# A scale by 1/sqrt(D) goes from a pass over a weight tile to ScalarE's evacuations, and two modulation rows go to two periods

## The chip, the cores and the metric

The kernel runs on one core of one Trainium2 chip. The metric is device time of one execution in microseconds (us), as the median of the timed runs. The program is one launch; the host only lays the inputs out.

The engines of the core are named as the profile names them: PE (TensorE matmuls), PEld (TensorE's weight loads), DVE (VectorE), ACT (ScalarE), POOL (GpSimd) and SP (SyncE, whose queue issues the DMAs here).

## The reference, cut to what matters

Two blocks run one after the other on x of shape 2 x 2048 x 512 (two sequences, L = 2048 positions, D = 512 features). The first is an S5 block with a feed-forward. The second is attention between two modulated layer norms, with 16 heads of 32 features. The change is in the second block alone:

```python
def _L1_cond_ref(hidden, w, ...):
    h = _sln(hidden, w, ln_g, ln_b, Wg, bg, Wb, bb)      # layer norm, then gamma * ln + beta
    q, k, v = split of (h @ Wqkv.T + bqkv) into 16 heads of 32
    energy = jnp.einsum('bhqd,bhkd->bhqk', q, k)
    att = jax.nn.softmax(energy, axis=-1) / D ** 0.5     # the 1/sqrt(D) stands after the softmax
    out = jnp.einsum('bhqk,bhkd->bhqd', att, v)
    out = out @ Wp.T + bp
    h1 = out + hidden
    h2 = _sln(h1, w, ln_g, ln_b, Wg, bg, Wb, bb)         # the same gamma and beta again
    return h2 + h1
```

So 1/sqrt(D), named ISQ in the kernel, is a plain factor on the attention's output. It may be multiplied in anywhere between the softmax and the projection by Wp. The last layer norm needs two rows of 512 numbers for each sequence: a scale (gamma times ln_g) and a shift (gamma times ln_b, plus beta).

## The kernel before

The first stage, up to about 1390 us, runs the S5 block and the feed-forward chunk by chunk, and computes keys, queries and values. The attention stage comes after it and fills the rest.

The attention stage handles 64 blocks. A block `n` is a sequence `b`, a pair of heads `p` and a chunk `c` of 512 queries. Each block has 16 key tiles of 128 keys, and scores are held transposed: keys along the partitions, 2 heads x 512 queries along the row. The softmax subtracts the true maximum of each query, so a block's maxima must be complete before its first exponential:

- `keep` (L867, L872): PE makes a score tile `s` in PSUM, ACT copies it to SBUF as `x`, and DVE takes the running maximum `run`. Eleven of the 16 tiles of a block are treated so. `compare` (L876) only takes the maximum of the other five.
- `turn_run` and `spread` (L884 to L898): the maxima are transposed on PE, reduced on DVE, sent to DRAM and read back spread over all partitions as `shift`.
- `take_off` (L904): POOL adds `shift` to each of the eleven kept tiles. `make` (L910): PE recomputes the five others, and DVE adds `shift`, giving `pT`.
- `exponentials` (L915): ACT takes the exponential of each tile, in place.
- `weighted` (L925): PE multiplies the exponentials with the values into one PSUM bank `o`. The weights hold the values and a block of ones, so rows 0 to 31 of `o` are the output of the even head, rows 32 to 63 its sum, rows 64 to 95 the sum of the odd head and rows 96 to 127 its output. After the last tile of a block ACT copies `o` to `raw` (L934), and SP writes the sums and the outputs to DRAM (`sd` at L938, `od` at L941). There are 63 such copies; the last block of all ends in `end_last` instead.

A hand-written order sets who follows whom: the program is recorded in periods `j`, eight to a block (`NP = 8`), and each engine executes its instructions in the order in which they were recorded. `after(j, ...)` puts a piece of work at the head of period `j`, `closing(j, ...)` puts it behind that period's exponentials. Scores run 14 periods ahead of their use (`AHEAD`). All DMAs go through SP's queue, in order.

What the change and the steps below it touch:

- `wp`, the projection's weights, is loaded in period 2 * NP + 6. In period 4 * NP (head of block 4) POOL multiplies the whole tile, 128 x 2048, by ISQ in place (L1328).
- `last_rows(b)` makes the two modulation rows of sequence `b` with `along_rows` (L170, L174): matmuls of a broadcast column against the identity into the PSUM bank "pt", then an ACT copy to SBUF. There is one "pt" bank, and `turn_run`, `spread` and the projections use it too. `last_rows` is called twice, by `after`: for the first sequence (`b` = 0) at the head of block 34, and for the second (`b` = LB) at the head of period `j + 2`, where `j` is the period after the one in which the last head pair's first chunk is complete.
- `fetch`, `divide`, `project`, `residual`, `statistics` and so on (L979 to L1080) take finished chunks through the division by the sums, the projection and the last norm. For the first sequence this is spread over the second sequence's blocks; for the second it comes at the end.
- `end_last` finishes the last block: its outputs go straight from PSUM to the projection without the way through DRAM. It divides by the sums with one reciprocal and two multiplications for each half (L1162, L1164).

Of the kernel before, what the change touches and what calls it, by code (L numbers as in the profile page):

```python
# [8 lines left out]
F32 = mybir.dt.float32  # L9
# [4 lines left out]
AF = mybir.ActivationFunctionType  # L14
# [5 lines left out]
P = 128  # L20
# [19 lines left out]
def tile_s5_block_then_sln_attention(  # L40
# [125 lines left out]
    def along_rows(dst, cols, psum, tag):  # L166

        pt = psum.tile([P, CH], F32, name="pt_ar", tag=tag)
        for k in range(KC):
            nc.tensor.matmul(  # L170
                pt[:, k * P : (k + 1) * P], cols[k].to_broadcast([P, P]), ident,
                start=True, stop=True,
            )
        nc.scalar.copy(dst, pt)  # L174
# [743 lines left out]
    def weighted(n, kt, first, final):  # L918

        if first:  # L920
            outs[n] = ps_o.tile([P, CH], F32, name="o")
        x = probs.pop((n, kt))
        v = vst[pair_of[n] % 2]
        for e in range(2):
            nc.tensor.matmul(  # L925
                outs[n][64 * e : 64 * e + 64, :], v[:, kt, e : e + 2, :], x[:, e, :],
                start=first, stop=final,
            )
        if final and n == len(blocks) - 1:
            end_last(outs.pop(n))  # L930
        elif final:
            b, p, c = blocks[n]
            raw = work.tile([P, CH], F32, name="raw", bufs=1)
            nc.scalar.copy(raw, outs.pop(n))  # L934
            cols = slice(c * CH, (c + 1) * CH)
            for e in range(2):
                j = 2 * p + e
                nc.sync.dma_start(sd[b][j : j + 1, cols], raw[32 + 32 * e : 33 + 32 * e, :])  # L938
            for e in range(2):
                j = 2 * p + e  # L940
                nc.sync.dma_start(od[b][HD * j : HD * j + HD, cols], raw[96 * e : 96 * e + 32, :])  # L941
# [1 line left out]

    held, ending = {}, {}

    def last_rows(b):
        g_row = rows.tile([P, D], F32, name="g_row", bufs=1)
        along_rows(g_row, [s_scale[:, k, b : b + 1] for k in range(KC)], ps, "pt")
        t_row = rows.tile([P, D], F32, name="t_row", bufs=1)
        along_rows(t_row, [s_shift[:, k, b : b + 1] for k in range(KC)], ps, "pt")  # L950
        ending[b] = g_row, t_row

    def fetch_sums(b, c, heads=slice(0, NH), width=64):

# [196 lines left out]
    def end_last(o):  # L1151
        raw, inv = (spare(n)[:, 0, :] for n in ("raw4", "inv4"))
        on = ends["o"][1][:, 1, :]
        turned = ps.tile([P, 2, 2 * P], F32, name="turned", tag="pt")
        parts = [slice(2 * i * P, 2 * (i + 1) * P) for i in range(2)]
        for at in parts:
            nc.scalar.copy(raw[:, at], o[:, at])
        end_begin(1)
        for i, at in enumerate(parts):
            nc.tensor.matmul(turned[:, i, :], ends["turn"], raw[:, at], start=True, stop=True)  # L1160
        for i, at in enumerate(parts):
            nc.vector.reciprocal(inv[:, at], turned[:, i, :])  # L1162
            for r in (slice(0, HD), slice(3 * HD, P)):
                nc.vector.tensor_tensor(on[r, at], o[r, at], inv[r, at], ALU.mult)  # L1164
        end_project(1, list(range(NG - 1)))
        mv = small.tile([P, TT, 2], F32, name="mv4")
        g_row, t_row = ending[LB]
        for i in range(2):
            for t in (2 * i, 2 * i + 1):
                nc.tensor.matmul(  # L1170
                    ends["py", i][:, t % 2, :], on[:, t * P : (t + 1) * P], ends["w"], start=False, stop=True
                )
            for t in (2 * i, 2 * i + 1):
                st = small.tile([P, 6], F32, name="st3")
                nc.vector.bn_stats(st, ends["py", i][:, t % 2, :])
                nc.vector.bn_aggr(mv[:, t, :], st)
        v = small.tile([P, TT], F32, name="v4")
        scale = small.tile([P, TT], F32, name="scale4")
        nc.vector.tensor_scalar(v, mv[:, :, 1], EPS, None, ALU.add)
        nc.vector.tensor_scalar(  # L1180
            scale.bitcast(I32), v.bitcast(I32), -0.5, float(0x5F3759DF), ALU.mult, ALU.add
        )

        nc.gpsimd.tensor_scalar(v, v, -0.5, None, ALU.mult)
        for _ in range(3):
            c = small.tile([P, TT], F32, name="c4")
            nc.gpsimd.tensor_tensor(c, scale, scale, ALU.mult)
            nc.gpsimd.tensor_tensor(c, c, v, ALU.mult)
            nc.gpsimd.tensor_scalar(c, c, 1.5, None, ALU.add)
            nc.gpsimd.tensor_tensor(scale, scale, c, ALU.mult)  # L1190
        ws, hts = [spare("w01"), spare("w23")], [spare("ht01"), spare("ht23")]
        for t in range(TT):
            h = ends["py", t // 2][:, t % 2, :]
            w, ht = ws[t // 2][:, t % 2, :], hts[t // 2][:, t % 2, :]
            nc.vector.scalar_tensor_tensor(w, h, mv[:, t, 0:1], g_row, ALU.subtract, ALU.mult)
            nc.vector.tensor_tensor(ht, h, t_row, ALU.add)
        for t in range(TT):
            qt = LC * TT + t
            w, ht = ws[t // 2][:, t % 2, :], hts[t // 2][:, t % 2, :]
            nc.vector.scalar_tensor_tensor(ht, w, scale[:, t : t + 1], ht, ALU.mult, ALU.add)  # L1200
            nc.sync.dma_start(out[LB, qt * P : (qt + 1) * P, :], ht)
# [47 lines left out]
    for b in range(NB):  # L1249
        for c in range(NQ):  # L1250
            j = NP * (blocks.index((b, NPAIR - 1, c)) + 1) + 1
            if (b, c) == (LB, LC):
                most, rest = slice(0, NH - 4), slice(NH - 4, NH - 2)
                j = NP * (N - 1)
                after(j - 5, fetch_sums, b, c, most)
                after(j - 3, invert, b, c, most)
                for g in range(NG - 1):
                    after(j - 2 + g, end_sums, g)
                after(j + 1, end_weights)
                after(j + 1, end_sums_more)  # L1260
                after(j + 2, end_x)
                after(j + 1, fetch_sums, b, c, rest, 32)
                after(j + 4, invert, b, c, rest, 32)
                after(j + 5, end_divisors, NG - 1, 2, 1)
                for g in range(NG - 1):
                    after(j + 3 + g, end_divide, g)
                for e in (1, 2):
                    after(j + 8, end_divide, NG - 1, slice(HD * e, HD * e + HD))
                after(j + 6, end_begin, 0)
                for g in range(NG - 1):  # L1270
                    after(j + 6 + g // 2, end_project, 0, [g])
                continue
            after(j, fetch_sums, b, c)
            after(j + 2, invert, b, c)
            if c == 0:
                after(j + 2, last_rows, b) if b == LB else after(NP * (NPAIR * NQ * (b + 1) + 2), last_rows, b)
            for t in range(TT):
                qt = c * TT + t
                if b == LB:
                    k = j + 3 + 2 * t  # L1280
                    after(k, fetch, b, qt)
                    after(k + 2, divide, b, qt)
                    after(k + 3, project, b, qt)
                    after(k + 3, residual, b, qt)
                    after(k + 3, statistics, b, qt)
                    after(k + 4, deviation, b, qt)
                    after(k + 5, last_norm, b, qt)
                    after(k + 6, last_close, b, qt)
                else:

                    k = NP * (NPAIR * NQ * (b + 1) + 2 + 3 * qt // 2)
                    after(k, fetch, b, qt)
                    after(k + 3, divide, b, qt)
                    for g in range(NG):
                        closing(k + 5 + g // 2, project, b, qt, (g,))
                    closing(k + 7, residual, b, qt)
                    closing(k + 8, statistics, b, qt)
                    closing(k + 9, gain, b, qt)
                    after(k + 11, turns, b, qt)
                    closing(k + 12, scaled, b, qt)  # L1300
                    after(k + 14, close, b, qt)
# [9 lines left out]
    for j in range(FIRST, NP * N + 2):  # L1311
# [12 lines left out]
            wp = fixed.tile([P, KC, D], F32, name="wp")  # L1324
        if j == 2 * NP + 6:
            nc.sync.dma_start(wp, w_pT.rearrange("(k p) f -> p k f", p=P))
        if j == 4 * NP:
            nc.gpsimd.tensor_scalar(wp, wp, ISQ, None, ALU.mult)  # L1328
        run_due(j)
        n, i = block_at(j + AHEAD)  # L1330
        todo = list(keeps[i]) if n is not None else []
# [90 lines left out]
```

## Time and profile before

| | |
|---|---|
| median of 3 runs | 3393.38 us (3393.34 to 3394.49) |
| the profiled execution | 3393.83 us |
| its span, first to last instruction | 3392.1 us |
| TensorE clock granted over the span | 0.992 |
| PE busy | 3294.7 us (97%) |
| POOL busy | 2117.6 us (62%) |
| ACT busy | 1951.0 us (58%) |
| DVE busy | 2218.2 us (65%) |
| the scale pass L1328 | 5.369 us, once, at 1531.7 us |
| a copy `raw` L934 | 588 ns, 63 times |
| an exponential L915 of a kept tile | 1059 ns, 704 times |
| a copy `x` L867 | 1011 ns, 704 times |
| an addition L904 on POOL | 2390 ns, 704 times |

The shares of busy time are means over two stages. In the first stage PE is busy and the other engines have much time to spare; in the attention stage all four compute engines are busy for most of each block. So the cost of an instruction is read from the stretch in which it stands. A steady block can be timed by the starts of two `raw` copies that follow each other: most of those of the first sequence are 28.1 us apart.

### The profile page before, as it was taken

How to read it: one execution, taken by the hardware profiler on the slowest of the kernel's cores; microseconds unless marked ns; L12 is line 12 of the kernel's file. 1: busy time of each engine (PE TensorE's matmuls, PEld its weight loads, DVE VectorE, ACT ScalarE, POOL GpSimd, SP SyncE). 2: the span in 40 equal slices, each digit the busy share in tenths (PEclk: the TensorE clock that was granted, in tenths of full speed). 3: DMA queues.
4: the chain of work that ended last, by engine and by line, in shares of the span. 5: the costliest groups of instructions: out<-in, count | busy, mean ns of one | idle time of the engine just before them, and what ended most of it. 6: DMA issues, size and time to landing. Idle time of an engine off the chain costs nothing.

```text
span 3392.1 us, 33637 instructions
## 1 busy us (share of the span) xinstructions
PE 3294.7 (97%) x11076; PEld 1417.8 (42%) x11076; DVE 2218.2 (65%) x2792; ACT 1951.0 (58%) x2210; POOL 2117.6 (62%) x1164
## 2 busy tenths in 40 slices
PE   7999999999999999999999999999999999999987
PEld 4444444444444444443444444444444434443432
DVE  5352525252525212688888888888888888888884
ACT  2111111111111111598999999999888888888852
POOL 2341313131313111399999999999899999989885
PEclk9999999999999999999999999999999999999998
DMA  8022221222222212332313231323233243243233
GB/s 298 25 50 71 53 75 49 78 57 71 62 62 56 59 47 75 113 85 61 74 49 74 67 74 49 75 68 75 70 92 90 67 95 88 65 90 83 63 102 97
DMA packets 249781, 259.07 MB, mean 76 GB/s; under 512 B 94920, under 2 KB 167112, under 8 KB 245510
## 3 DMA queue, kind: packets, MB, share of 16 engines
q1 hardware_dynamic: 249606, 256.92, 28.5%
q8 instruction: 88, 1.44, 0.2%
q14 instruction: 87, 0.71, 0.1%
HBM read 166.77 MB, written 67.76 MB: 69 GB/s over the span
## 4 chain that ended last, share of the span: by engine, by line
PE 62%; DVE 15%; ACT 15%; issue 3%; POOL 2%; DMA 2%; SPq 0%; DVEq 0%; ACTq 0%; POOLq 0%
PE ph L538 13%; PE po L551 13%; PE o L925 10%; DVE run L872 8%; PE s L856 8%; ACT x L867 7%; PE pk L587 6%; ACT x L915 4%; ACT pT L915 4%; PE pv L599 3%; DVE pT L910 3%; PE py L1005 2%; POOL x L904 2%; DVE run L876 2%; PE pu L474 2%
## 5 line engine op out<-in xcount | busy, mean ns | idle before, releaser
L904 POOL TENSOR_TENSOR x<-x,shift 128x1024 f32<-128x1024 f32 x704 | 1654.9, 2390 | 134.1 <-DMA shift<-flat 117.1
L856 PE MATMUL s<-qs,ks 128*128 128x512 f32 x2688 | 824.8, 427 | 39.4 <-DVE run L872 26.6
L867 ACT COPY x<-s 128x1024 f32<-128x1024 f32 x704 | 692.2, 1011 | 142.9 <-PE s L856 137.1
L872 DVE TENSOR_TENSOR run<-s,run 128x1024 f32<-128x1024 f32 x576 | 705.2, 1224 | 81.7 <-ACT x L867 37.1
L915 ACT ACTIVATE x<-x 128x1024 f32<-128x1024 f32 x704 | 738.8, 1059 | 15.7 <-POOL x L904 15.4
L925 PE MATMUL o<-x,v 128*64 128x512 f32 x2816 | 717.2, 611 | 1.2 <-ACT x L915 1.2
L856 PEld LDWEIGHTS s<-qs,ks 128*128 128x128 f32 x2688 | 444.1, 189 | 454.7 <-DVE run L872 158.0
L538 PE MATMUL ph<-fT,w_sb 128*128 128x512 f32 x1024 | 459.4, 592 | 0.9 <-ACT fT L682 0.9
L551 PE MATMUL po<-w_sb,hid 128*128 128x512 f32 x1024 | 460.0, 592 | 0.0
L542 ACT ACTIVATE hid<-ph,vec 128x512 f32<-128x512 f32 x128 | 87.8, 686 | 614.7 <-PE ph L538 614.7
L910 DVE TENSOR_TENSOR pT<-s,shift 128x1024 f32<-128x1024 f32 x320 | 388.9, 1215 | 52.6 <-PE s L856 52.2
L876 DVE TENSOR_TENSOR run<-s,run 128x1024 f32<-128x1024 f32 x320 | 389.3, 1216 | 12.1 <-PE s L856 11.6
L915 ACT ACTIVATE pT<-pT 128x1024 f32<-128x1024 f32 x320 | 339.5, 1061 | 89.9 <-DVE pT L910 89.6
L561 POOL TENSOR_TENSOR x<-x,gated 128x512 f32<-128x512 f32 x32 | 39.6, 1269 | 506.5 <-DVE gated L560 506.5
L925 PE MATMUL o<-pT,v 128*64 128x512 f32 x1280 | 332.0, 597 | 15.2 <-ACT pT L915 15.2
L164 DVE SCALAR_TENSOR_TENSOR lo<-pk,vec,hi 128x512 fp32r<-128x512 f32 x64 | 47.8, 746 | 423.0 <-ACT hi L163 423.0
L551 PEld LDWEIGHTS po<-w_sb,hid 128*128 128x128 f32 x1024 | 194.4, 190 | 243.9 <-issue 243.7
L538 PEld LDWEIGHTS ph<-fT,w_sb 128*128 128x128 f32 x1024 | 194.1, 190 | 243.3 <-issue 239.2
L925 PEld LDWEIGHTS o<-x,v 128*64 128x64 f32 x2816 | 157.0, 135 | 311.7 <-issue 239.3
L163 ACT ACTIVATE hi<-pk,vec 128x512 fp32r<-128x512 f32 x64 | 44.0, 687 | 373.4 <-PE pk L587 373.4
L524 POOL TENSOR_TENSOR x<-x,gated 128x512 f32<-128x512 f32 x28 | 35.4, 1264 | 255.3 <-DVE gated L523 255.3
L925 PEld LDWEIGHTS o<-pT,v 128*64 128x64 f32 x1280 | 91.6, 138 | 200.2 <-issue 142.2
(280 smaller groups left out, 2449.3 us busy)
## 6 DMA issues: line engine op xcount, KB each, us to landing
ks<-kd SPq DMA_DIRECT2D x128, 256.0 KB
qs<-qd SPq DMA_DIRECT2D x512, 64.0 KB
shift<-flat SPq DMA_DIRECT2D x64, 512.0 KB
moved<-fT SPq DMA_DIRECT2D x224, 64.0 KB
x<-in_x SPq DMA_DIRECT2D x8, 1024.0 KB
w_sb<-in_w SPq DMA_DIRECT2D x8, 1024.0 KB
kd<-hi SPq DMA_DIRECT2D x32, 256.0 KB
kd<-lo SPq DMA_DIRECT2D x32, 256.0 KB
```

The costliest lines, as they stand in the source:

```text
L538: nc.tensor.matmul(ph, w1_sb[:, k, f * P : (f + 1) * P], fts[b, c][:, k, :], start=k == 0, stop=k == KC - 1)
L551: nc.tensor.matmul(pos[b, c][:, t, :], hid[:, t * P : (t + 1) * P], w2_sb[:, f, :], start=f == 0, stop=f == FC - 1,)
L587: nc.tensor.matmul(pk, w[:, k, g * P : (g + 1) * P], hT[:, k, :], start=k == 0, stop=k == KC - 1)
L599: nc.tensor.matmul(pv, fts[b, c][:, k, t * P : (t + 1) * P], wv[:, k, :], start=k == 0, stop=k == KC - 1)
L856: nc.tensor.matmul(s[:, e, :], kst[pair_of[n], e][:, kt * P : (kt + 1) * P], qst[n][:, e, :], start=True, stop=True,)
L867: nc.scalar.copy(x, s)
L872: nc.vector.tensor_tensor(runs[n], s, kept[n, 0] if kt == 1 else runs[n], ALU.max)
L876: nc.vector.tensor_tensor(runs[n], raw_scores(n, kt), runs[n], ALU.max)
L904: nc.gpsimd.tensor_tensor(x, x, shifts[n], ALU.add)
L910: nc.vector.tensor_tensor(x, s, shifts[n], ALU.add)
L915: nc.scalar.activation(x, x, AF.Exp)
L925: nc.tensor.matmul(outs[n][64 * e : 64 * e + 64, :], v[:, kt, e : e + 2, :], x[:, e, :], start=first, stop=final,)
```

## The change

Three things are done.

1. The pass of POOL over `wp` (L1328) is taken out. A column `by_row` of 128 numbers takes its place: ISQ on the 64 partitions that hold outputs, 1.0 on the 64 that hold sums. ACT's evacuation of `o` to `raw` becomes an activation Identity with `by_row` as its scale, one factor for each partition. POOL fills the column once, with three memsets.
2. `end_last`, which does not pass through `raw` for its outputs, multiplies by ISQ in its division: `scalar_tensor_tensor` in place of `tensor_tensor`, four times.
3. `last_rows` becomes `last_row`, which makes one row. The two rows are recorded behind the exponentials of two successive periods by `closing`, no more both at the head of one by `after`. For the second sequence they also come up to two periods earlier (`j` and `j + 1`, where it was `j + 2`).

```diff
@@ weighted
-            nc.scalar.copy(raw, outs.pop(n))
+            nc.scalar.activation(raw, outs.pop(n), AF.Identity, scale=by_row)
@@
-    def last_rows(b):
-        g_row = rows.tile([P, D], F32, name="g_row", bufs=1)
-        along_rows(g_row, [s_scale[:, k, b : b + 1] for k in range(KC)], ps, "pt")
-        t_row = rows.tile([P, D], F32, name="t_row", bufs=1)
-        along_rows(t_row, [s_shift[:, k, b : b + 1] for k in range(KC)], ps, "pt")
-        ending[b] = g_row, t_row
+    by_row = small.tile([P, 1], F32, name="by_row", bufs=1)
+    nc.gpsimd.memset(by_row, ISQ)
+    for i in (1, 2):
+        nc.gpsimd.memset(by_row[HD * i : HD * i + HD], 1.0)
+
+    def last_row(b, name, columns):
+        row = rows.tile([P, D], F32, name=name, bufs=1)
+        along_rows(row, [columns[:, k, b : b + 1] for k in range(KC)], ps, "pt")
+        ending.setdefault(b, []).append(row)
@@ end_last
-                nc.vector.tensor_tensor(on[r, at], o[r, at], inv[r, at], ALU.mult)
+                nc.vector.scalar_tensor_tensor(
+                    on[r, at], o[r, at], ISQ, inv[r, at], ALU.mult, ALU.mult
+                )
@@ the plan
-                after(j + 2, last_rows, b) if b == LB else after(NP * (NPAIR * NQ * (b + 1) + 2), last_rows, b)
+
+                k = j if b == LB else NP * (NPAIR * NQ * (b + 1) + 2)
+                closing(k, last_row, b, "g_row", s_scale)
+                closing(k + 1, last_row, b, "t_row", s_shift)
@@ the loop over periods
-        if j == 4 * NP:
-            nc.gpsimd.tensor_scalar(wp, wp, ISQ, None, ALU.mult)
```

## The prediction

> **What bounds the kernel now.** I read the page first, then the windows from one `raw` copy to the next, then the timeline at each of the three places that the change touches, and last the groups by form for durations. From the page:
>
> ```profile
> span 3392.1 us, 33637 instructions
> PE 3294.7 (97%) x11076; PEld 1417.8 (42%) x11076; DVE 2218.2 (65%) x2792; ACT 1951.0 (58%) x2210; POOL 2117.6 (62%) x1164
> ```
>
> The shares of POOL and ACT hide that the attention stage loads all four engines. The windows show it (columns: stretch, length, then PE, PEld, DVE, ACT and POOL busy, granted clock, DMA share, GB/s):
>
> ```profile
> 1506.66:1534.79 28.13, 27.83 (x116) 11.54 (x115) 24.76 (x23) 26.66 (x31) 26.25 (x11) 1.00 0.14 43
> 1534.79:1567.76 32.97, 29.00 (x118) 11.51 (x116) 24.76 (x23) 26.62 (x30) 29.48 (x13) 1.00 0.38 90
> 1567.76:1596.09 28.33, 27.68 (x115) 11.36 (x114) 24.75 (x23) 26.62 (x30) 27.67 (x13) 1.00 0.20 55
> ...
> 2357.60:2388.94 31.34, 30.36 (x134) 13.51 (x132) 24.75 (x23) 27.84 (x32) 30.16 (x14) 1.00 0.26 69
> ```
>
> A normal block takes 28.13 us with PE busy for 27.83, ACT for 26.66 and POOL for 26.25 of them. So a few microseconds put into one engine's order in one place cannot be made up: they move the end. The second and fourth rows are two blocks in which that happens.
>
> **Part 1, the pass over wp.** The timeline at the second row:
>
> ```profile
> 1526.85 4.74 POOL L904 TENSOR_TENSOR x<-x,shift 128x1024 f32<-128x1024 f32 x2 [1.80 <-DMA shift<-flat]
> ...
> 1531.68 5.37 POOL L1328 TENSOR_SCALAR wp<-wp 128x2048 f32<-128x2048 f32 x1
> ...
> 1537.13 21.08 POOL L904 TENSOR_TENSOR x<-x,shift 128x1024 f32<-128x1024 f32 x9
> ...
> 1539.53 1.06 ACT L915 ACTIVATE x<-x 128x1024 f32<-128x1024 f32 x1 [4.16 <-POOL x L904]
> ```
>
> POOL cannot start a block before its shift lands, and the pass sits behind the second of eleven additions. Without it the third would end at 1531.59 + 2.38 = 1533.97; its exponential, one block (28.13) after that of 1507.12, would be due at 1535.25. So POOL has 1.28 to spare, and the pass costs 5.37 - 1.28 = 4.1: ACT's idle 4.16. With the refilling of the pipeline the block is 32.97 - 28.13 = 4.84 longer, and the next 28.33 - 28.13 = 0.20, part of which other blocks with key loads show too (28.35 at 1905.51). Gain 4.95. What is late next at that place is PE, as in any block. The Trainium skill (GPSIMD Engine Reference, section 4.1) calls one-input elementwise work on GpSimd "roughly line-rate"; with its 128 fp32 a cycle (section 3) and 1.2 GHz that is an estimate of 2048 / 1.2 = 1.7 us for this pass, so a delay of only 0.4, and the whole sum below would be 3.6. The row says 5.369 and ACT's wait confirms it, so I take the trace.
>
> **Part 2, the rows.** Before, both at once:
>
> ```profile
> 2381.71 1.16 PE L170 MATMUL pt_ar<-ident,s_scale 128*128 128x128 f32 x8
> 2382.91 0.59 ACT L174 COPY g_row<-pt_ar 128x512 f32<-128x512 f32 x1 [0.90 <-PE pt_ar L170]
> 2383.55 1.16 PE L170 MATMUL pt_ar<-ident,s_shift 128*128 128x128 f32 x8 [0.68 <-ACT g_row L174]
> 2384.46 1.63 PE L856 MATMUL s<-qs,ks 128*128 128x512 f32 x6
> ...
> 3200.23 1.16 PE L170 MATMUL pt_ar<-ident,s_scale 128*128 128x128 f32 x8 [1.29 <-DVE neg L885]
> ...
> 3202.98 1.62 PE L856 MATMUL s<-qs,ks 128*128 128x512 f32 x6
> ```
>
> The second row needs the one "pt" bank, so PE stands until ACT has copied the first. First pair: PE gives 2384.46 - 2381.71 = 2.75 to it, and the block is 31.34 - 28.13 = 3.21 longer. Second pair: it stands behind `turn_run`, whose bank DVE still reads, so PE waits for that as well; the scores of 3202.98 would have begun 0.41 after the transposes of 3198.28, so PE loses 4.29. Some returns: from the `raw` before it to `pt_neg` it is 3210.24 - 3191.89 = 18.35, and in a block with the same reciprocal (L963) 2315.44 - 2300.56 = 14.88. Excess 3.47.
>
> After, by the program's order, the first row stands behind six scores and the second behind the next block's first six (for LB, behind the six and then the four of two successive periods). No wait is left: the bank's earlier users are periods away, and the first row's copy is recorded before `raw`, ahead of the second row's matmuls. What stays is PE's work, 2384.46 - 2383.55 = 0.91 for a row, since the row is eight records and not the transposes' four. ACT's copy, 0.46 from start to start, lies beside it. In the first pair about 0.3 of the first row vanishes in PE's own waits for DVE at the block's end (0.23 at 1507.53 in a normal block); the rest falls where PE ends last. So 1.5 stays in the first pair and 1.8 in the second: gains 3.21 - 1.5 = 1.7 and 3.47 - 1.8 = 1.7. The price of a row lies between 0.46 (only ACT's copy shows) and 1.3 (both add up), so each gain between 0.7 and 2.5.
>
> **Part 3, 63 evacuations with a factor.** No row has this form. The nearest:
>
> ```profile
> 1506.66 0.58 ACT L934 COPY raw<-o 128x512 f32<-128x512 f32 x1
> 1507.12 1.08 ACT L915 ACTIVATE x<-x 128x1024 f32<-128x1024 f32 x1
> ...
> 1508.36 1.01 ACT L867 COPY x<-s 128x1024 f32<-128x1024 f32 x1 [0.16 <-PE s L856]
> ...
> L1053 ACT ACTIVATE o<-o,scale 128x512 f32<-128x512 f32 x16 | 11.5, 722 | 0.0
> L1072 ACT ACTIVATE z<-xr,shift,scale 128x512 f32<-128x512 f32 x12 | 9.3, 779 | 3.2 <-DVE neg L885 3.1
> ```
>
> L1053 has the same function and a scale by partition, from SBUF: 722 ns, and 0.61 to the next start (2468.59 to 2469.20). The copy takes 588, and 0.46 to the next. So +0.14 by 63, 8.8 us more of ACT; upper bound L1072 with two columns, 0.72 to the next, +0.26; lower bound nothing. Is it on the path? The exponential behind `raw` is used a period later. The copy behind that waits 0.16 for PE, and back-to-back ACT instructions overlap by about 0.1 here, so it has about 0.25 to spare. PE's next product into `o` starts at 1508.20, and `raw` is done at 1507.24. So +0.14 is hidden; in a few blocks (2482.15) the copy follows at once, and I charge 0.1 in all. At +0.26 little would show either. The rule that speaks against the change is in the Trainium skill (ScalarE: Activation LUTs, What ACT_TABLE_LOAD costs): each [128,1] pointer operand adds about 93 ns. Over 63 that is 5.9 us, and with ACT as the limit the sum would be 2.2. The idle 0.16 before the copy decides for hidden. The function needs no table load: the program's order has three loads before and after.
>
> **The small rest.** `end_last`'s four multiplications are on the final chain: 742 (L1047, this form) against 681 (L1048, the old one) for 512 columns, so at most 0.24; I take 0.2, not below nothing. The memsets are three of 0.10 (L1413) in a POOL order that stands 49.07 us idle before L1323: nothing, 0.3 if that cover were gone. The writes of `sd` and `od` go out 0.14 later, and on SP's queue the query loads behind them, which run blocks ahead: nothing. SP's and DVE's orders are else unchanged. The projection now waits for wp's load (issued 1495.3) and not for POOL, first at 2404: nothing. `by_row` slides the SBUF tiles behind it by 32 bytes; L915 takes 1059 on `x`, whose tiles start at odd multiples of 32, and 1061 on `pT`, at multiples of 64: nothing.
>
> **The sum.** -4.95 - 1.7 - 1.7 + 0.1 + 0.2 = -8.05 against the profiled execution's 3393.83 (3392.1 of span and 1.7 around it). That execution is 0.45 above the median and inside the runs' range; so from the median 3393.38 it gives 3385.3.
>
> **The rivals.** (a) ACT is the limit after all, and the longer `raw` comes through. For: ACT is back to back from `pT` to the next copies in each block. Against: the idle before the copy. At 0.09 to 0.14 each it gives 5.7 to 8.8 back: 3391.0 to 3394.1, within 0.2%. (b) Splitting the rows saves nothing, since PE's work is the same and the restart is paid twice. For: ACT's copy of the second row lies where DVE waits 2.06 for ACT's copies. Against: 0.68 and 1.29 us of waits go. Then -4.95 + 0.3: 3388.7. (c) Slower: the evacuation costs more than any near row shows, say by reading `o` from PSUM with a factor. The place is the copy behind the exponential; beyond 0.25 more than the copy each extra counts 63 times. It cancels the gain at 0.25 + 8.05 / 63 = 0.38 and is slower by over 0.2% from 0.49; at 0.5 it is +15.8 - 8.05, so 3401.1. For: no row has the form. Against: PSUM rows with two columns (L156) take 778 to 811 ns.
>
> **How the numbers follow.** 0.2% is 6.8 us, about what a measurement of this kernel can tell from no change. The sum is likeliest, 0.74, with a range of its own of 3383 to 3388 (part 2's bounds and 0.3 on part 1): 0.64 of it below 3386.6 and 0.10 above. (a) has 0.10, (b) 0.09, (c) 0.07. The range 3382.5 to 3390.5 takes in the sum's range, (b) and a small part of (a), and leaves out (c). Faster 0.64, within 0.2% 0.29, slower 0.07.
>
> **What would show it.** Right: L1328 gone; the `raw` starts at 1534.79 and the next about 28.1 apart; no wait of PE for `g_row`, and eight records of L170 in four places without idle before them; `raw` at 690 to 720 ns, with the copy two places behind it still waiting for PE. Wrong: blocks of the first sequence 0.1 longer than 28.13 throughout with that idle gone (a); the blocks with rows still above 30.5 (b); `raw` above 900 ns (c).

## The result: 3384.49 us, and the profile after

The changed kernel takes 3384.49 us as the median of 8 runs (3382.16 to 3387.56), and the kernel before takes 3393.36 us beside it (8 runs, 3390.28 to 3397.74). The ratio is 0.9977, with a 95% interval of 0.9968 to 0.9987. That is 8.87 us less, where the prediction's sum was 8.05 us less. The profiled execution of the change, the fastest of the eight, took 3382.16 us, with a span of 3380.4.

From the page of the change:

```profile
span 3380.4 us, 33642 instructions
PE 3285.9 (97%) x11076; PEld 1416.0 (42%) x11076; DVE 2217.5 (66%) x2792; ACT 1957.1 (58%) x2210; POOL 2111.1 (62%) x1166
```

PE, PEld and DVE execute as many instructions as before. ACT has gained 6.1 us, which is 63 evacuations at 0.103 each (6.5) to within half a microsecond. POOL has two instructions more, three memsets for one pass. The shares of busy time have hardly moved, so again they say nothing of where the time went.

The windows from one `raw` to the next say it. The columns are stretch, length, then PE, PEld, DVE, ACT and POOL busy, granted clock, DMA share, GB/s. The second and fourth rows are the two blocks that were 32.97 and 31.34 long:

```profile
1504.35:1532.45 28.10, 27.78 (x116) 11.54 (x115) 24.73 (x23) 26.74 (x30) 26.68 (x12) 1.00 0.15 43
1532.45:1560.58 28.13, 27.84 (x116) 11.55 (x115) 24.59 (x23) 26.75 (x30) 25.17 (x12) 1.00 0.48 116
1560.58:1588.86 28.28, 27.81 (x116) 11.55 (x115) 24.92 (x23) 26.73 (x30) 26.36 (x12) 1.00 0.15 45
2349.94:2378.51 28.57, 28.26 (x123) 12.23 (x122) 25.21 (x23) 27.20 (x31) 26.77 (x12) 1.00 0.29 73
2378.51:2410.47 31.96, 31.96 (x133) 14.70 (x134) 24.98 (x24) 27.27 (x32) 29.91 (x14) 1.00 0.39 79
3181.74:3217.07 35.33, 33.72 (x139) 14.90 (x138) 27.57 (x36) 27.71 (x32) 31.93 (x15) 1.00 0.35 103
```

Before, the windows of the last two of these blocks read:

```profile
2388.94:2420.39 31.45, 30.80 (x123) 12.94 (x122) 25.35 (x24) 26.65 (x30) 27.16 (x13) 1.00 0.39 80
3191.89:3228.84 36.95, 33.82 (x139) 14.84 (x138) 27.64 (x36) 27.62 (x33) 30.61 (x15) 1.00 0.36 98
```

Below, a block's number is that of the `raw` copy at its end, counted from 1 (the kernel counts from 0), so these are blocks 5, 34, 35 and 61. Block 5 has lost 32.97 - 28.13 = 4.84. Blocks 34 and 35 together have lost 62.79 - 60.53 = 2.26: one row of the pair has moved into block 35, which is 0.51 longer, and block 34 is 2.77 shorter. Block 61 has lost 1.62. From the first `raw` to the 62nd it is 1826.11 before (1450.06 to 3276.17) and 1816.64 after (1447.77 to 3264.41): 9.47 less, of which these three places are 8.72.

Not all of the 4.84 is the pass. The prediction saw 4.16 of idle time on ACT in block 5 and took the other 0.68 for the refilling of the pipeline. The end of that block before, in ACT's and then in SP's timeline, shows another cause:

```profile
1564.04 1.06 ACT L915 ACTIVATE x<-x 128x1024 f32<-128x1024 f32 x1 [0.86 <-POOL x L904]
```

```profile
1553.83 0.27 SPq L896 DMA_DIRECT2D flat<-neg_row  x1
1556.99 0.34 SPq L898 DMA_DIRECT2D shift<-flat  x1
```

The read `shift` of the next block goes out 3.16 us after the write `flat`. The usual gap is 1.3 (median of 64 in this trace). So POOL's next additions came late in this one execution, and ACT waited for them once more. Three other runs told below keep the pass and have no late read there; in them block 5 is 31.91 to 32.22, and the pass costs 3.8 to 4.1.

What lies ahead of the first `raw` is not the change either. POOL's first instruction of the attention stage, the memset of `v`, starts at 1405.59 before and at 1403.44 after, with the same work in the same order ahead of it, but for the three short memsets of `by_row`. The first 100 us differ in the clock column, before and then after:

```profile
0.00:100.00 100.00, 79.19 (x367) 46.12 (x368) 58.70 (x231) 22.78 (x34) 22.91 (x40) 0.93 0.70 254
```

```profile
0.00:100.00 100.00, 78.83 (x372) 45.67 (x373) 58.94 (x231) 23.36 (x35) 25.10 (x42) 0.95 0.71 256
```

By this column the twelve traces of this document fall into two groups, whatever the kernel. In six it is 0.93, and the memset of `v` starts at 1405.6 to 1407.2; in six it is 0.95 to 0.97, and the memset starts at 1403.4 to 1404.0. That the clock is the cause is likely but not shown. The run of the change that is told last below had 0.93, and its first `raw` at 1449.90, as before. So of the 11.7 us between the two spans some 7.7 are the change, some 2 are the first stage, 1.05 is the late read, and the rest is small.

Where the pass stood, POOL now goes on with its additions (the timeline of POOL, then of ACT, in the change):

```profile
1524.42 21.17 POOL L904 TENSOR_TENSOR x<-x,shift 128x1024 f32<-128x1024 f32 x9 [1.42 <-DMA shift<-flat]
...
1533.03 1.07 ACT L915 ACTIVATE x<-x 128x1024 f32<-128x1024 f32 x1
```

Nine additions follow each other behind the landing of `shift`. The exponential of the third, which waited 4.16 us for POOL, comes directly behind `raw` with no idle time at all.

The two rows of the first pair, in PE's timeline of the change:

```profile
2374.04 1.65 PE L856 MATMUL s<-qs,ks 128*128 128x512 f32 x6
2375.53 1.05 PE L170 MATMUL pt_ar<-ident,s_scale 128*128 128x128 f32 x8
2376.52 1.08 PE L925 MATMUL o<-x,v 128*64 128x512 f32 x4
...
2379.89 1.05 PE L170 MATMUL pt_ar<-ident,s_shift 128*128 128x128 f32 x8
2380.87 1.94 PE L925 MATMUL o<-x,v 128*64 128x512 f32 x8
```

Each row takes 0.98 to 0.99 from its start to PE's next work, and neither has idle time before it. In the second pair there is one new wait, of a transposition for the bank that ACT is still reading:

```profile
3189.64 0.59 ACT L174 COPY t_row<-pt_ar 128x512 f32<-128x512 f32 x1
...
3190.28 0.66 PE L884 MATMUL pt_run<-ident,run 128*128 128x128 f32 x4 [0.28 <-ACT t_row L174]
```

The evacuation, from the list of the tile `raw` on ACT (min/median/max in ns):

```profile
L934 ACT ACTIVATE raw<-o,by_row x63: 668/691/713, 1447.8 to 3307.1; 128x512 f32<-128x512 f32 x63
```

### The profile page after: what moved, and what is told of

Same layout as the page of the kernel before. It is cut to its first block, busy times and chain, and to the rows that moved or that the text cites. A ratio compares the mean times of both kernels' runs of the same rounds, so it can differ in the third digit from the quotient of the medians.

```text
span 3380.4 us, 33642 instructions
## 1 busy us (share of the span) xinstructions
PE 3285.9 (97%) x11076; PEld 1416.0 (42%) x11076; DVE 2217.5 (66%) x2792; ACT 1957.1 (58%) x2210; POOL 2111.1 (62%) x1166
## 4 chain that ended last, share of the span: by engine, by line
PE 62%; ACT 16%; DVE 13%; DMA 3%; issue 3%; POOL 2%; SPq 1%; ACTq 0%; DVEq 0%; POOLq 0%
PE ph L538 13%; PE po L551 13%; PE o L925 10%; PE s L856 8%; DVE run L872 7%; ACT x L867 7%; PE pk L587 7%; ACT x L915 5%; ACT pT L915 4%; PE pv L599 3%; DVE pT L910 2%; PE py L1008 2%; POOL x L904 2%; PE pu L474 2%; DVE run L876 2%
```

## The experiments

Two theories stood against each other on most points. The sum's theory: the gain is a stall of ACT behind POOL's pass, plus PE's waits for the one "pt" bank, and the longer evacuation is hidden by ACT's idle time. Against it: the evacuation is on the path and takes gain back, the split of the rows is worth nothing, or what looks like a gain comes from addresses or from the run.

### One part alone: the pass without the rows

The change without its third part: `last_rows` and its two calls stand as before.

> The change without its rows: the pass over wp gone, the factor in the evacuations and in end_last, both rows as before in one period. If the pass costs what ACT's wait showed: raw intervals like before except the one of 32.97, which falls to 28.1, so -4.9 to -5.1 us against before; the blocks with rows stay at 31.3 and 36.9. If the gain came from the rows alone: 0. If the longer evacuation is on the path: blocks of 28.2 to 28.3 throughout and only about +1 to +4 us against before.

It took 3389.07 us (21 runs), where the kernel before took 3392.79 (49 runs): 0.9988 (0.9982 to 0.9995). Block 5 is 28.12, as in the change, and the blocks with rows are 31.33 and 36.95, as before. So the stall in block 5 goes with the pass alone, and the median's 3.7 us is what the pass costs where no late read comes on top of it (3.8). The 4.9 to 5.1 that were expected had taken the late read in.

### The other part alone: the rows, with the pass kept

Before, with `last_row` and its `closing` calls:

> The rows alone: two periods, the pass over wp and the plain copies kept. If the rows gain by the waits that go (for the one bank, and for VectorE behind turn_run): -3.4 to -3.9 us against before, with the interval of 32.97 still there. If splitting saves nothing because TensorE's work is the same: 0, within 0.5.

It took 3389.20 us (21 runs) against the same 3392.79: 0.9987 (0.9981 to 0.9994), 3.6 us less. Blocks 34, 35 and 61 are 28.57, 31.95 and 35.34, the change's lengths to 0.01. The pass is still there, and its stall reads (POOL, then ACT):

```profile
1530.12 5.37 POOL L1329 TENSOR_SCALAR wp<-wp 128x2048 f32<-128x2048 f32 x1
...
1537.98 1.06 ACT L915 ACTIVATE x<-x 128x1024 f32<-128x1024 f32 x1 [4.27 <-POOL x L904]
```

Block 5 is 32.22, so the stall is 4.10 here. The two parts measured alone add to 3.7 + 3.6 = 7.3, and together they gave 8.9. With intervals of 2 us and more on either side of each figure this is no sign of an interplay, and the blocks show none.

### The evacuation with a factor, and nothing else

Before, with only the new form of the evacuation, and a column that holds ones everywhere, so that the pass stays:

```diff
-            nc.scalar.copy(raw, outs.pop(n))
+            nc.scalar.activation(raw, outs.pop(n), AF.Identity, scale=by_row)
+    by_row = small.tile([P, 1], F32, name="by_row", bufs=1)
+    nc.gpsimd.memset(by_row, 1.0)
```

> The evacuation alone: Identity with a column of ones as its factor in place of the copy; pass and rows as before, so the output is the reference's. If the longer evacuation is hidden behind the next copy's wait for TensorE: raw at 690 ns, all raw intervals within 0.05 of before, 0 us, at most +0.5. If ScalarE is the limit: +0.1 in each of 63 intervals, +6 to +9 us.

It took 3392.32 us (13 runs) against 3392.79: 0.9999 (0.9991 to 1.0007). All blocks but the fifth have the length that they have before, to about 0.05, save blocks 18, 38, 56 and 63 (by 0.15 to 1.2, three of them shorter); in these four, runs with the plain copy differ from that trace of before too. So 63 evacuations, each 103 ns longer, cost nothing that can be measured. If ACT were the limit it would be 63 times 0.11, some 6.9 us, or 0.20%, outside the interval. The fifth block is 31.91 here, with the whole pass in it and ACT's wait for POOL at 3.86:

```profile
1529.44 5.38 POOL L1331 TENSOR_SCALAR wp<-wp 128x2048 f32<-128x2048 f32 x1
...
1537.31 1.06 ACT L915 ACTIVATE x<-x 128x1024 f32<-128x1024 f32 x1 [3.86 <-POOL x L904]
```

The stall is 31.91 - 28.13 = 3.78, and the wait alone is all of it. There is nothing left over for a refilling.

### The evacuation twice: how much cover there was

The change, with each evacuation executed twice:

```diff
-            nc.scalar.activation(raw, outs.pop(n), AF.Identity, scale=by_row)
+            for _ in range(2):
+                nc.scalar.activation(raw, outs[n], AF.Identity, scale=by_row)
+            outs.pop(n)
```

> The changed kernel with each evacuation done twice into the same tile, the second a repeat. One more costs ScalarE 0.57 us a block. If the slack behind the evacuation is what is left of about 0.25 us, here some 0.1 to 0.15: each interval longer by 0.4 to 0.5, +26 to +30 us against the changed kernel. If ScalarE has slack of more than half a microsecond in each block: 0. If it has none: +0.57 by 63, +36 us.

It took 3407.62 us (5 runs): 1.0039 (1.0026 to 1.0052) of before, and 23.1 above the change's median, a little less than was expected. Most blocks of the first sequence are 0.55 longer than in the change (28.66 for 28.11), and that is more than was expected of each. In the second sequence those of 31.4 and of 28.1 are longer by about as much; those of 32.6 and 29.2 are not longer at all. In all, 44 blocks are longer by 0.36 to 0.70 and 17 are not longer; block 63, which differs by over 1 us between traces anyway, is left out. So the total came near because two misses cancelled.

The place can be read from ACT's timeline, of the change and then of this kernel:

```profile
1504.35 0.69 ACT L934 ACTIVATE raw<-o,by_row 128x512 f32<-128x512 f32 x1
1504.92 1.07 ACT L915 ACTIVATE x<-x 128x1024 f32<-128x1024 f32 x1
...
1506.06 1.01 ACT L867 COPY x<-s 128x1024 f32<-128x1024 f32 x1
```

```profile
1507.81 1.41 ACT L935 ACTIVATE raw<-o,by_row 128x512 f32<-128x512 f32 x2
1509.12 1.05 ACT L915 ACTIVATE x<-x 128x1024 f32<-128x1024 f32 x1
1510.07 1.00 ACT L867 COPY x<-s 128x1024 f32<-128x1024 f32 x1
...
1511.10 1.23 DVE L872 TENSOR_TENSOR run<-s,run 128x1024 f32<-128x1024 f32 x1 [0.20 <-ACT x L867]
...
1514.83 1.23 DVE L872 TENSOR_TENSOR run<-s,x 128x1024 f32<-128x1024 f32 x1 [2.50 <-ACT x L867]
...
1516.11 0.73 PE L856 MATMUL s<-qs,ks 128*128 128x512 f32 x2 [0.31 <-DVE run L872]
```

Back to back, the copy starts 0.95 after the exponential (1509.12 to 1510.07). In the change it starts 1.14 after it (1504.92 to 1506.06), so there are still 0.19 us in which ACT could be later; before, with 1507.12 to 1508.36, there were 0.29. The change has used 0.11 of the 0.29. The second evacuation adds 1.31 - 0.57 = 0.74 and can hide 0.19 of it, which leaves the 0.55 that each block shows. Behind it the delay goes from ACT's copies to DVE's maxima: the next one waits 0.20 for its copy, where the change has no such wait, and the one at 1514.83 waits 2.50, where it waits 2.06 in the change. PE's scores then wait 0.31 for that maximum, and in the change they do not wait there. So the cover in the first sequence is real, it has a size, and it is small.

### Both rows in one period

The change, with the second row in the first one's period:

```diff
-                closing(k + 1, last_row, b, "t_row", s_shift)
+                closing(k, last_row, b, "t_row", s_shift)
```

> The changed kernel with both rows in the first of its two periods, one behind the other; all else as changed. If the gain comes from the two periods, TensorE again stands until ScalarE has copied the first row, here behind ScalarE's longer queue: +1.5 to +5 us against the changed kernel, all of it in the intervals that hold the rows (28.57 and 31.96, and 35.33). If only the place matters, away from turn_run: those three intervals stay within 0.3.

It took 3388.93 us (21 runs), where the kernel before took 3393.24 (43 runs): 0.9991 (0.9984 to 0.9997). That is 4.3 less by the medians and 3.1 by the ratio, so about the pass alone. Blocks 34 and 35 together take 63.16, 0.37 more than before, and block 61 takes 37.19, 0.24 more. PE's timeline of it:

```profile
2377.49 1.05 PE L170 MATMUL pt_ar<-ident,s_scale 128*128 128x128 f32 x8
2380.64 1.16 PE L170 MATMUL pt_ar<-ident,s_shift 128*128 128x128 f32 x8 [2.10 <-ACT g_row L174]
```

The move from the head of a period to its end brings nothing by itself. It makes PE's wait longer, 2.10 for 0.68, since ACT's copy of the first row is recorded behind two copies and an exponential there. All of the gain of the third part comes from the split in two periods. The split alone, at the heads of two periods and not behind their exponentials, was not run.

### Both pairs elsewhere

The change, with the rows put where PE has idle time: those of the first sequence ahead of the first block, those of the second six periods later, when the last blocks no longer have scores ahead of them to make in full.

```diff
-                k = j if b == LB else NP * (NPAIR * NQ * (b + 1) + 2)
+                k = j + 6 if b == LB else -2
```

> The changed kernel with the rows moved to where TensorE waits: the first sequence's before the first exponentials (periods -2 and -1), the second's to j + 6 and j + 7, behind its first projection. If a row's price of about 0.9 us of TensorE is paid only where TensorE is the engine that ends last: intervals 34 and 35 come to 28.1 and 31.4, interval 61 to about 33.5, and the beginning at most 0.5 later; -2.5 to -3.5 us against the changed kernel. If the price is paid wherever they stand: 0.

It took 3384.05 us (7 runs): 0.9972 (0.9960 to 0.9983), not to be told from the change; the 2.5 to 3.5 less that were expected did not come. Blocks 34 and 35 without any row are 28.13 and 31.42 long, so together 59.55. This measures what the first pair costs, and no other run does: it cost 62.79 - 59.55 = 3.24 before, and costs 60.53 - 59.55 = 0.98 in the change, 0.44 in one block and 0.54 in the other. Blocks 61 and 62 are 34.65 and 46.79 for 35.33 and 47.34, together 1.23 less. Against these 2.2 us stands the stretch from POOL's memset of `v` to the first `raw`: 46.11, where it is 44.47 before and 44.33 in the change, and 45.47 at most in any other trace. So the first pair's rows cost between 0.6 and 1.8 at the new place, against the 0.98 that they saved.

### An unused column of 32 bytes

Before, with a column that nothing reads, so that the tiles behind it are moved as in the change:

```diff
+    pad = small.tile([P, 1], F32, name="pad", bufs=1)
+    nc.gpsimd.memset(pad, 1.0)
```

> The kernel before with one unused column of 32 bytes in the place of by_row, so that the SBUF tiles behind it lie 32 bytes further on, as in the changed kernel; nothing else. If the slide costs and gains nothing: 0, within 0.05%, and all raw intervals as before. If the 2.3 us by which the changed kernel's first stage was shorter came from it: -2 us, all before the first raw.

It took 3392.38 us (13 runs) against 3393.24: 0.9999 (0.9991 to 1.0007). Block 5 is 31.92 and the blocks with rows 31.34 and 36.96. So the addresses cost and gain nothing that the blocks show, or the times to 0.1%. The first `raw` does come at 1448.22 here, 1.84 earlier than before, as it should if the addresses mattered. But the rows alone and the pass in four pieces, in which nothing is moved, have it at 1448.40 and 1448.35, and these traces too are of the group with the higher clock in the first 100 us.

### The pass in four pieces

Before, with 512 columns of the pass at the head of each of blocks 4 to 7 (counted from 0 as in the kernel, so that their lengths are those of blocks 5 to 8 here):

```diff
-        if j == 4 * NP:
-            nc.gpsimd.tensor_scalar(wp, wp, ISQ, None, ALU.mult)
+        if j % NP == 0 and 4 <= j // NP < 8:
+            g = j // NP - 4
+            nc.gpsimd.tensor_scalar(wp[:, g, :], wp[:, g, :], ISQ, None, ALU.mult)
```

> The kernel before with the pass over wp cut in four pieces of 512 columns, one at the head of each of blocks 4 to 7; copies and rows as before. If the pass cost what it did because 5.37 us in one place is more than GpSimd has to spare there (1.28), a piece of about 1.35 costs 0 to 0.2: interval 5 falls to 28.1 to 28.3 and the next three are within 0.2 of before, -4 to -4.8 us. If GpSimd's work is paid for wherever it stands: 0 against before.

It took 3391.09 us (13 runs) against 3393.24: 0.9994 (0.9986 to 1.0002), so by the times alone no difference is shown, and the 4 to 4.8 less that were expected did not come. The trace shows a difference. Blocks 5 to 8 are 28.11, 29.40, 28.12 and 28.37 long, where the change has 28.13, 28.28, 28.12 and 28.12. Two pieces cost nothing, one costs 0.25 and one 1.12: 1.4 in all, in place of 3.8 to 4.1. POOL's timeline has the first two pieces, and ACT's the wait behind the second:

```profile
1524.88 4.73 POOL L904 TENSOR_TENSOR x<-x,shift 128x1024 f32<-128x1024 f32 x2 [1.45 <-DMA shift<-flat]
1529.70 1.49 POOL L1329 TENSOR_SCALAR wp<-wp 128x512 f32<-128x512 f32 x1
...
1554.40 4.75 POOL L904 TENSOR_TENSOR x<-x,shift 128x1024 f32<-128x1024 f32 x2 [1.96 <-DMA shift<-flat]
1559.24 1.49 POOL L1329 TENSOR_SCALAR wp<-wp 128x512 f32<-128x512 f32 x1
...
1563.23 1.06 ACT L915 ACTIVATE x<-x 128x1024 f32<-128x1024 f32 x1 [1.47 <-POOL x L904]
```

A piece moves the next addition by 1529.70 to 1531.28, or 1.58. The prediction gave POOL 1.28 to spare in block 5, in a trace in which the block's first addition starts 7.94 ahead of the `raw` at 1534.79. Here it starts 8.18 ahead of the one at 1533.06, which leaves 1.52, and the piece vanishes. In block 6 `shift` lands later against ACT's order, and the first addition starts 6.77 ahead of the `raw` at 1561.17. That leaves 0.11, and the other 1.47 of the piece is what ACT waits. So a block's spare time on POOL is not one number: the landing of `shift` sets it anew each time.

### The last pair alone, later, and the change again

Of the two moves told above, only the one that gained, on one chip with a second run of the change:

```diff
-                k = j if b == LB else NP * (NPAIR * NQ * (b + 1) + 2)
+                k = j + 6 if b == LB else NP * (NPAIR * NQ * (b + 1) + 2)
```

> The change with only the second sequence's two rows put later, at the ends of periods j + 6 and j + 7 instead of j and j + 1; the first sequence's rows stay as in the change. If a row's price is PE's work and PE has idle time near the end, the raw intervals 61 and 62 should fall as they did with both pairs moved (35.33 to about 34.65, and 47.34 to about 46.8), intervals 34 and 35 stay at 28.57 and 31.96, and the first raw comes as early as in the change: about 1.2 us less than the change, so about 3383.3. If the 1.2 us only moved within the tail, it is given back behind the last raw and the time is the change's, 3384.5.

> The change as it is, again, on the chip of the run beside it. Every theory expects 3384.5 and a ratio of 0.9977 to the kernel before. Raw intervals 5, 34, 35 and 61 at 28.13, 28.57, 31.96 and 35.33 if what was read from one trace holds for another; the first stage and the last three intervals may differ by some 2 us if they vary with the granted clock from run to run.

With the last pair later it took 3382.97 us (7 runs), 0.9971 (0.9960 to 0.9982) of the 3393.62 that the kernel before took there (16 runs). The change again took 3385.99 (10 runs), 0.9978 (0.9968 to 0.9987). The intervals overlap, so the times do not show that the one is faster than the other; the median is 3.0 lower, more than the trace accounts for. The traces show 1.22: blocks 61 and 62 take 34.65 + 46.81 for 35.34 + 47.34. Behind them nothing is given back that can be told: from the 62nd `raw` to the end it is 116.1, where the two traces of the change have 116.0 and 117.5. The median of 3382.97 is the lowest of all kernels that were run. The second run of the change has blocks 5, 34, 35 and 61 at 28.11, 28.57, 31.94 and 35.34, so what was read from one trace holds for the other.

## Why the prediction was right, point by point

- **The pass (4.95 predicted).** It is worth 3.8 to 4.1. The step itself, the pass less what POOL had to spare, gave 4.1 and was right. The term that was mis-sized is the one added to it, 0.68 for the refilling and 0.2 for the block behind: the first was no refilling but the 0.86 us stall behind a late read of `shift`, which stood in the profiled execution and in none of the others at this block, and the second is in the change's block 6 as well (28.28). The trace had the line for it, some 30 us behind the pass's start. The block of 28.35 at 1905.51, named for the second, is no example either: it takes 28.11 in the change. The weighing of page and row held: at the estimate of 1.7 us the pass would have been worth a few tenths (and the whole sum 3.5, not 3.6), and alone it gave 3.7.
- **The rows, first pair (1.7 predicted).** It gave 2.26. Before, the pair cost 3.24 (predicted 3.21). After, it costs 0.98, where the working left 1.5. This is the term that was mis-sized. The row itself was put at 0.91 of PE's time and takes 0.98, a little more; but of the two rows' 1.96 about half does not come through, and not 0.3 of one row only. Part of it is seen: in block 35 PE is idle for 0.29 in the run with both pairs elsewhere, and for nothing in the change. Where the rest goes was not followed.
- **The rows, second pair (1.7 predicted).** It gave 1.62. The split, and not the earlier place, is what brought it. Its two terms, 3.47 before and 1.8 after, are not shown: in every run both rows of this pair stand in block 61, so that only the difference is measured. "No wait is left" was not quite right: the transposition of the maxima now waits 0.28 for ACT's copy of the second row.
- **The evacuation (+0.1 predicted, 690 to 720 ns each).** It takes 691 ns, or 103 more than the copy, near the 93 that the prediction quotes for one more operand; and alone it changed nothing measurable. The estimate of 0.25 for what the copy has to spare was near: 0.29. The sign that the prediction named could not serve: the 0.16 of idle before the copy is no longer listed in the change, and still the copy has 0.19 to spare, because the start of one ACT instruction overlaps the end of the one before.
- **The small rest (+0.2 predicted).** It was nothing: the four multiplications with a factor take what the four without it took (0.85 and 0.86 us a pair), at 256 columns on 32 partitions. The memsets (104 and twice 91 ns) lie at 1338, in POOL's idle stretch. The 32 bytes cost nothing.
- **The rivals.** (a) ACT as the limit fell by the run with the factor alone, and its threshold was measured by the run with two evacuations. (b) The split being worth nothing fell by the run with both rows in one period, which is what (b) would have looked like: 3388.93, where (b) said 3388.7. (c) fell by the 691 ns; that ACT's extra time does make this kernel slower beyond its cover, the run with two evacuations shows.

The terms as the blocks have them give -3.8 (to -4.1) - 2.26 - 1.62 = -7.7 to -8.0 with nothing added, where the sum had -8.05: an excess of 0.9 to 1.2 on the pass was cancelled by 0.5 too little on the rows and 0.3 of charges that were not due. The mechanism was right in each part; that the sum was near to a few tenths is luck. The medians differ by 8.87, and the interval of the ratio reaches from 4.4 to 10.9 us.

## What to carry to other kernels

A longer instruction in the middle of a queue costs what it adds, less the time to spare until its next consumer is due. Read that time from the starts of the two neighbours: the cover of 0.29 us on ACT here hid an edit of 0.11 sixty-three times, and would not have hidden one of 0.74; and on POOL it was not one number, but changed from block to block with the landing of `shift`. Where two short pieces of work share one buffer, split them so that each one's reader finishes under other work; here moving the pair together gained nothing, and the split gave all of it. Take the price of a block from two neighbouring starts in the trace where the effect is under the spread of the times, and first look in that block for anything that other executions do not have.

## What the runs showed of the hardware

The read-back of the maxima through DRAM is late about once in an execution, at a place that changes, which I had not expected. In SP's queue the gap between `flat` and `shift` is 1.3 us in the median of each trace. Leaving out the last blocks, where it reaches 4.6 to 5.3 in every trace, it is 3.0 to 3.6 once in nine of the twelve traces and never in three. Four times it stands in block 17, twice in block 29, and once each in 5, 19 and 31. In the run with the last pair later it came in block 17:

```profile
1890.03 0.27 SPq L896 DMA_DIRECT2D flat<-neg_row  x1
1893.47 0.34 SPq L898 DMA_DIRECT2D shift<-flat  x1
```

Blocks 17 and 18 took 29.70 and 29.48 there, in place of 28.11 each, which is 3.0 us. Only the 1.6 of block 17 is like the other traces, in which the two blocks at the late read are longer by 0.1 to 1.6 together. In block 18 of this trace, and of no other, the granted clock fell to half for 3.4 us:

```profile
1906.60:1909.90 3.30, 3.30 (x9) 0.82 (x6) 2.39 (x3) 2.87 (x4) 3.30 (x2) 0.50 0.55 131
```

PE had just waited 0.96 and 0.60 for DVE's maxima there; whether that made the clock fall is not shown. The order of the queue is the same in all traces; what makes the write 2 us late was not found. Beside the granted clock of the first 100 us (0.93 to 0.97) it is one reason why executions of one kernel lie several us apart, and why the times alone do not tell the change from its two variants with rows moved.

One-input work on POOL was no cheaper than two-input work: the pass took 5.37 us for 2048 columns, or 2.6 ns each, in pieces 1.49 us for 512, or 2.9 ns each; an addition of two tiles takes 2.39 us for 1024, or 2.3 ns each. At one shape, 128x512, the first stage of the kernel before has 1.49 and 1.55 us for two such multiplications by a number (L397, L398) and 1.27 for a multiplication of two tiles (L511).
